# A first-pass weight product as a 2x3 by 3x3 block product in 15 products instead of a 2x2 by 2x2 one in 7, with chained banks and a ring of operands

## The chip, the cores and the metric

The kernel runs on one core of a Trainium2 chip. The metric is the device time of one execution in microseconds, taken on the chip; the profile is of one execution by the hardware profiler. The engines are named PE (TensorE), DVE (VectorE), ACT (ScalarE), POOL (GpSimd) and SP (SyncE, here only a queue for transfers).

## The reference

The input is 128 graphs of 64 nodes with 768 features each, and an adjacency matrix of whole numbers per graph. Two layers follow each other, each of the form x = x + layer(relu(layernorm(x))).

```python
def layer0(h, adj):
    radj = swapaxes(adj, 1, 2)
    deg, rdeg = adj.sum(-1), radj.sum(-1)          # zeros replaced by 1 in the divisions
    ctx = (adj @ (h @ Wadj.T + badj)) / deg
    ctx = ctx + (radj @ (h @ Wrev.T + brev)) / rdeg
    ctx = ctx + h @ Wself.T + bself
    agg = einsum('bij,bijr->bir', adj, E[adj])     # E[rels] with rels = adj
    rel = agg @ Wr.T + br * deg
    rr = where(radj + 40 > 40, radj + 40, 0)
    ragg = einsum('bij,bijr->bir', radj, E[rr])
    return ctx + rel + ragg @ Wrr.T + brr * rdeg

def layer1(h, adj):                                # six heads of 128
    z = einsum('bni,hio->bhno', h, W)
    a = leaky(src(tanh(z)) + dst(tanh(z)).T)       # masked where adj == 0
    f = elu(softmax(a) @ z + b)
    g = sigmoid(h @ H_w.T + H_b)
    return g * f + (1 - g) * h
```

Layer 0 has three 768x768 products for every node (Wadj, Wrev, Wself). They dominate the first pass, and they are what the change rewrites.

## The kernel before, in words

Two graphs make a tile of 128 rows by 768 columns; there are 64 tiles, handled in NP = 32 pairs. A first pass does layer 0 for all pairs, a second pass layer 1; between them h of layer 1 and x + h go through memory (H1D and XH1).

**Operands of the first pass.** For each tile, layernorm and relu give h (ACT, L331). TensorE multiplies blocks of h by the graph's matrices A/deg, Aᵀ/rdeg and the identity (L422, output in PSUM under the name pb), so that the features come out transposed, with nodes in columns, as a left operand for the three weights. ACT copies these blocks from PSUM to SBUF (L434, L440). All three weights are summed into the same PSUM bank, so a product of one row block with one column block is a chain of matmuls over (block of the inner dimension, weight).

**The product before.** Per pair the two tiles are two row blocks, and the 768 inner rows and 768 columns are each halved. This 2x2 by 2x2 block product is done in Winograd's form with 7 products instead of 8. Each product is KH = 3 inner blocks times 3 weights = 9 matmuls of 128x384 in fp32 (L466), so 63 for a pair, which the trace shows as 126 records (an fp32 matmul leaves two). Four banks, pwa to pwd, take them. The sums of operands that the form wants are s1 and s3 by DVE (L441, L442, one input still in PSUM) and s2 and s4 by POOL (L447, L452); the sums of weights, twelve tiles of 1152 columns, are made once at the start by DVE (L184). DVE adds every finished bank to x (L483, eight adds of 128x384 a pair).

**Counts.** The relation terms depend only on how often each value is found in a row of the adjacency matrix. DVE compares (L378), masks (L383) and reduces (L385), makes digits (L390 to L396), POOL copies them (L401), TensorE transposes them (L409), ACT copies those (L411), and a short bf16 matmul with a table (L475) adds the relation terms to the banks.

**End of a pair.** finish(p) runs beside the next pair's products: statistics by DVE (L159 to L165), a power on POOL (L166), the small DVE operation L167 for the second factor, relu by ACT to hf (L524), the store of hf, x + hf by POOL (L526), the store of x.

**Order of the work.** main(p) lists a pair's matmuls as numbered steps. side(p+1) lists the next pair's preparation with step numbers, and merged() issues each side piece at its number; the scheduler of the framework then settles the order on each engine. Each engine works its own queue in order and waits on the others by semaphores. Buffers are taken from rings: x and h1 share one ring of eight tiles of 128x768. fetch() brings the second pass's weights during the last pair of the first pass.

**Second pass.** Transposes of h (L646), seven products with two weights (L675), the attention (L753, L810, L819, L835), and the final L849 to L852.

Of the kernel before, what the change touches and what calls it, by code (L numbers as in the profile page):

```python
# [15 lines left out]
P = 128  # L16
EPS = 1e-5
NEG_MASK = -999.0
LEAKY = 0.2


@with_exitstack
def kernel(
# [47 lines left out]

    nc = tc.nc
# [11 lines left out]
    HALF = D // 2  # L84
    HH = H // 2
# [9 lines left out]
    assert GT == 2 and N == 64 and DO == P and H == KB and KB % 2 == 0 and H % 2 == 0  # L95
# [76 lines left out]
    def block(name, mats, place):  # L172
        return [keep.tile([P, KH, HALF], F32, name=f"{name}{s}", tag=f"w{place}{s}") if s < 2 else
                keep.tile([P, KH, HALF], F32, name=f"{name}{s}", tag="wl", bufs=7)
                for s in range(mats)]


    SUMS = {"T1": ("T3", "11"), "T2": ("22", "T1"), "T4": ("21", "T2"), "T3": ("22", "T3")}

    def sum_of_weights(w, to, behind=False):  # L180

        a, b = SUMS[to]
        for s, t in enumerate(w[to]):
            ins = nc.vector.tensor_sub(t, w[a][s], w[b][s])  # L184
            if behind:
                tc.keep_in_program_order(ins)


    bv, H1 = {}, {}

    def load_h(p):
        for k in range(2):
            t = 2 * p + k
            H1[t] = keep.tile([P, D], F32, name="h1", tag="x", bufs=8)
            nc.sync.dma_start(H1[t], H1D[p][k * P : (k + 1) * P, :])

    def fetch():

        def blk_of(name, place, h, q):
            bv[name] = block(f"bv{name}", 2, place)  # L200
            for s, src in enumerate((w_cat, hw_t)):
                nc.sync.dma_start(
                    bv[name][s],
                    src[h * HALF : (h + 1) * HALF, q * HALF : (q + 1) * HALF].rearrange(
                        "(k p) n -> p k n", p=P))

        def own(name, place):
            bv[name] = block(f"bv{name}", 2, place)

        return [(4, lambda: load_h(0)),  # L210
                (9, lambda: blk_of("11", "11", 0, 0)),
                (19, lambda: blk_of("21", "21", 1, 0)),
                (28, lambda: blk_of("T3", "T1", 0, 1)),
                (37, lambda: blk_of("22", "T2", 1, 1)),
                (47, lambda: (own("T1", "T4"), sum_of_weights(bv, "T1"), sum_of_weights(bv, "T3"))),
                (58, lambda: (own("T2", "T3"), sum_of_weights(bv, "T2")))]


    with ExitStack() as px:
# [7 lines left out]
        def load(p):  # L227
# [7 lines left out]
            for t in (2 * p, 2 * p + 1):  # L235
                X[t] = keep.tile([P, D], F32, name="x", bufs=8)
                nc.sync.dma_start(X[t], xf[t * P : (t + 1) * P, :])

        load(0)
# [3 lines left out]
        bia = work.tile([5, D], F32, name="bia", tag="s3")  # L243
        for i, v in enumerate((br, brr, badj, brev, bself)):
            nc.scalar.dma_start(bia[i : i + 1, :], row(v, 1))


        bw = {n: block(f"bw{n}", 3, n) for n in ("11", "21", "22", "T1", "T2", "T3", "T4")}

        def load_block(to, h, q):  # L250
            for s, src in enumerate((wadj_t, wrev_t, wself_t)):
                nc.sync.dma_start(
                    to[s], src.rearrange("(k h p) n -> h p k n", h=2, p=P)[h][:, :, q * HALF : (q + 1) * HALF])

        load_block(bw["11"], 0, 0)
        load(1)
        load_block(bw["21"], 1, 0)
        load_block(bw["T3"], 0, 1)
        load_block(bw["22"], 1, 1)
        wrt = work.tile([P, 2, D], F32, name="wrt", tag="a1")  # L260
        nc.sync.dma_start(wrt[:, 0, :], wr_t)
        nc.sync.dma_start(wrt[:, 1, :], wrr_t)
# [22 lines left out]
        def build_table():  # L285
# [21 lines left out]
            for hf in range(2):  # L307
                s = slice(hf * HALF, (hf + 1) * HALF)
                for d in range(2):
                    nc.tensor.matmul(pt[:NROW, hf, :HALF], es[:, d, :], wrt[:, d, s],  # L310
                                     start=(d == 0), stop=False)
                nc.tensor.matmul(pt[:NROW, hf, :HALF], eb, bia[:, s], start=False, stop=True)
            v = work.tile([P, D], F32, name="tv", tag="eq", bufs=1)
            qs = work.tile([P, 3, D], BF16, name="tq", tag="a22")
            nc.scalar.copy(v[:NROW].rearrange("p (a b) -> p a b", a=2), pt[:NROW, :, :HALF])
            for i in range(3):
                q = qs[:, i]
# [7 lines left out]
        A1, A22, S1, S2, S3, S4 = {}, {}, {}, {}, {}, {}  # L325
# [87 lines left out]
        def operands(p, k, q):  # L413
# [12 lines left out]
            pv = ps[:, :, : 6 * N].rearrange("p g (x n) -> p g x n", n=N)  # L426

            def blocks(ap):
                return ap.rearrange("p s (g n) -> p g s n", g=GT)

            if k == 0:
                if q == 0:
                    A1[p] = work.tile([P, KH, 2, 3, P], F32, name="a1")
                nc.scalar.copy(A1[p][:, q].rearrange("p h s (g n) -> p g (h s) n", g=GT), pv)  # L434
                return
            if q == 0:
                A22[p] = work.tile([P, KH, 3, P], F32, name="a22")
                S1[p] = work.tile([P, KH, 3, P], F32, name="s1", bufs=1)
                S3[p] = work.tile([P, KH, 3, P], F32, name="s3")
            nc.scalar.copy(blocks(A22[p][:, q]), pv[:, :, 3:])  # L440
            nc.vector.tensor_sub(blocks(S3[p][:, q]), blocks(A1[p][:, q, 0]), pv[:, :, :3])  # L441
            nc.vector.tensor_add(blocks(S1[p][:, q]), blocks(A22[p][:, q]), pv[:, :, :3])  # L442

        def sum2(p):
            S2[p] = work.tile([P, KH, 3, P], F32, name="s2", bufs=1)
            for q in range(KH):
                nc.gpsimd.tensor_sub(S2[p][:, q], S1[p][:, q], A1[p][:, q, 0])  # L447

        def sum4(p):
            S4[p] = work.tile([P, KH, 3, P], F32, name="s4", bufs=1)  # L450
            for q in range(KH):
                nc.gpsimd.tensor_sub(S4[p][:, q], A1[p][:, q, 1], S2[p][:, q])  # L452

        def main(p):

            bank = {}
            x0, x1 = X[2 * p], X[2 * p + 1]
            steps = []

            def mm(b, a, w, first):  # L460
                for q in range(KH):
                    for s in range(3):
                        def step(q=q, s=s):
                            if first and q == s == 0:
                                bank[b] = psw.tile([P, 512], F32, name=f"pw{b}")
                            nc.tensor.matmul(bank[b][:, :HALF], a()[:, q, s, :], bw[w][s][:, q, :],  # L466
                                             start=(first and q == s == 0),
                                             stop=(q == KH - 1 and s == 2),
                                             skip_group_check=True)
                        steps.append(step)  # L470

            def counts(b, k, q):
                def step():
                    for i, (a, e) in enumerate(PARTS):
                        nc.tensor.matmul(bank[b][:, :HALF], CT_T[p, k][: 3 * (e - a), i, :],  # L475
                                         tabs[i][:, q * HALF : (q + 1) * HALF],
                                         start=False, stop=True, skip_group_check=True)
                steps.append(step)

            def add(xt, q, b):  # L480
                def step():
                    v = xt[:, q * HALF : (q + 1) * HALF]
                    nc.vector.tensor_add(v, bank[b][:, :HALF], v)  # L483
                last = steps[-1]
                steps[-1] = lambda: (last(), step())

            mm("a", lambda: A1[p][:, :, 0], "11", True)
            add(x0, 0, "a")
            mm("c", lambda: A1[p][:, :, 1], "21", True)
            if p:  # L490
                counts("c", 0, 0)
                add(x0, 0, "c")
            mm("b", lambda: S1[p], "T1", True)
            add(x1, 1, "b")
            mm("a", lambda: S2[p], "T2", False)
            add(x0, 1, "a")
            mm("d", lambda: A22[p], "T4", True)
            if p:
                counts("d", 1, 0)
                add(x1, 0, "d")  # L500
            mm("a", lambda: S3[p], "T3", False)
            add(x1, 0, "a")
            mm("b", lambda: S4[p], "22", False)
            n = len(steps)
            counts("a", 1, 1)
            add(x1, 1, "a")
            if p:
                steps.insert(n - 4, steps.pop())
            else:
                counts("c", 0, 0)  # L510
                add(x0, 0, "c")
                counts("d", 1, 0)
                add(x1, 0, "d")
            counts("b", 0, 1)
            add(x0, 1, "b")
# [13 lines left out]
        def side(p):  # L529

            if p >= NP:
                return []
            return [(4, lambda: load(p + 1)),
# [3 lines left out]
                    (6, lambda: prep_r(p)),  # L537
                    (10, lambda: count(p, 0)),
                    (18, lambda: operands(p, 0, 0)),
# [424 lines left out]
```

## Time and profile before

| what | value |
|---|---|
| time before, median of 3 | 2593.01 us (2592.85 to 2593.08) |
| span of the profiled execution | 2591.5 us |
| busy: PE, DVE, ACT, POOL | 2543.7, 1765.7, 856.6, 733.4 us |
| from one pair to the next, first pass | 47.36 us |
| from one pair to the next, second pass | 31.66 us |
| start of pair 1 of the first pass | 89.88 us |
| first transpose of the second pass | 1554.08 us |

The busy figures are sums over the whole span and over stages with different limits. The period of a pair is taken from the starts of the first product in the chain of waits, and the last two rows divide the span into the start-up with pair 0, the 31 other pairs of the first pass, and the second pass. Where a matmul is followed by another, its time on TensorE is best read from start to start, as the records overlap.

### The profile page before, as it was taken

The page shows a single profiled execution, that of the slowest core. Times are in us where ns is not written, and L with a number is a line of the kernel's source. Part 1 is how long each engine was busy: PE and PEld are TensorE (multiplying, and loading weights), DVE is VectorE, ACT ScalarE, POOL GpSimd, SP SyncE. Part 2 cuts the span into 40 slices and gives each one's busy share as a digit, 9 for nine tenths or more (in the row PEclk, how much of TensorE's full clock was granted, in tenths as well). Part 3 has the DMA queues.
Part 4 walks back from the last instruction along what each step waited for, and adds up shares of the span by engine and source line. Part 5 has one row for each costly group of instructions (what it writes and reads, how often), then busy time and mean ns, then how long its engine had stood idle before and what let it go on. Part 6 is the DMA issues. An engine that isn't in the chain of part 4 may idle for free.

```text
span 2591.5 us, 31957 instructions
## 1 busy us (share of the span) xinstructions
PE 2543.7 (98%) x10924; PEld 1525.5 (59%) x10924; DVE 1765.7 (68%) x3887; ACT 856.6 (33%) x2596; POOL 733.4 (28%) x1055
## 2 busy tenths in 40 slices
PE   6999999999999999999999999999999999999996
PEld 3556666556566565565665655656566565565654
DVE  7856566565564665655655435888888888888888
ACT  1111112111111121111111104555555555555555
POOL 2331232232222312322223114333333333333332
PEclk9999999999999999999999999999999999999998
DMA  5112121121121111211211133333333333333322
GB/s 182 44 48 69 39 74 43 39 78 39 39 78 39 61 56 39 78 39 39 78 39 44 67 116 97 106 105 108 105 105 106 103 100 101 100 100 101 100 87 80
DMA packets 101572, 198.78 MB, mean 77 GB/s; under 512 B 35114, under 2 KB 43677, under 8 KB 101410
## 3 DMA queue, kind: packets, MB, share of 16 engines
q1 hardware_dynamic: 101256, 196.70, 23.9%
q8 instruction: 86, 1.41, 0.2%
q14 instruction: 76, 0.62, 0.1%
q10 hardware_dynamic: 154, 0.06, 0.0%
HBM read 95.67 MB, written 75.50 MB: 66 GB/s over the span
## 4 chain that ended last, share of the span: by engine, by line
PE 94%; DVE 3%; DMA 1%; ACT 1%; issue 1%; POOL 0%; SPq 0%; DVEq 0%; ACTq 0%; POOLq 0%
PE pwa L466 21%; PE pwb L466 14%; PE pma L675 14%; PE pmb L675 10%; PE pmc L675 9%; PE pwd L466 7%; PE pwc L466 7%; PE pb L422 5%; PE ps L835 2%; PE ps L646 2%; PE ps L819 1%; PE pwc L475 0%; DMA bw<-in_wadj_t_dram 0%; DVE bwT L184 0%; DMA x<-in_x_dram 0%
## 5 line engine op out<-in xcount | busy, mean ns | idle before, releaser
L466 PE MATMUL pwa<-bwT,s 128*128 128x384 f32 x1152 | 392.5, 490 | 0.4 <-DVE x L483 0.4
L466 PEld LDWEIGHTS pwa<-bwT,s 128*128 128x128 f32 x1152 | 215.5, 190 | 145.9 <-issue 8.0
L675 PE MATMUL pma<-bvT,s 128*128 128x384 f32 x768 | 279.4, 486 | 0.0
L447 POOL TENSOR_TENSOR s<-s,a 128x384 f32<-128x384 f32 x96 | 95.5, 1021 | 644.2 <-PE pwa L466 597.1
L483 DVE TENSOR_TENSOR x<-pwa,x 128x384 f32<-128x384 f32 x128 | 69.5, 543 | 206.8 <-PE pwa L466 170.7
L753 POOL TENSOR_TENSOR pr<-th,wsd 128x768 f32<-128x768 f32 x64 | 119.5, 1867 | 299.8 <-ACT th L751 236.6
L434 ACT COPY a<-pb 128x768 f32<-128x768 f32 x96 | 73.7, 801 | 392.3 <-PE pb L422 392.3
L466 PE MATMUL pwb<-bw,s 128*128 128x384 f32 x576 | 201.5, 489 | 0.0
L466 PE MATMUL pwb<-bwT,s 128*128 128x384 f32 x576 | 199.0, 491 | 0.0
L466 PE MATMUL pwa<-bw,a 128*128 128x384 f32 x576 | 196.2, 489 | 0.0
L466 PE MATMUL pwc<-bw,a 128*128 128x384 f32 x576 | 191.3, 486 | 0.0
L466 PE MATMUL pwd<-bwT,a 128*128 128x384 f32 x576 | 191.3, 486 | 0.0
L411 ACT COPY cntT<-pb 117x128 bf16<-117x128 bf16 (+1 forms) x128 | 27.8, 269 | 484.4 <-PE pb L409 484.4
L675 PEld LDWEIGHTS pma<-bvT,s 128*128 128x128 f32 x768 | 140.0, 190 | 80.8 <-DVE z L701 0.2
L422 PE MATMUL pb<-r,h 64*128 64x192 f32 x1536 | 153.8, 339 | 13.2 <-ACT h L331 6.7
L422 PEld LDWEIGHTS pb<-r,h 64*128 64x128 f32 x1536 | 124.5, 189 | 71.0 <-issue 52.9
L466 PEld LDWEIGHTS pwc<-bw,a 128*128 128x128 f32 x576 | 109.4, 190 | 76.6 <-issue 0.6
L466 PEld LDWEIGHTS pwd<-bwT,a 128*128 128x128 f32 x576 | 109.4, 190 | 76.3 <-issue 0.2
L675 PE MATMUL pmb<-bv,s 128*128 128x384 f32 x384 | 150.7, 502 | 0.0
L466 PEld LDWEIGHTS pwa<-bw,a 128*128 128x128 f32 x576 | 106.7, 191 | 69.4 <-issue 8.4
L466 PEld LDWEIGHTS pwb<-bwT,s 128*128 128x128 f32 x576 | 106.1, 190 | 69.1 <-issue 6.7
L675 PE MATMUL pmb<-bvT,s 128*128 128x384 f32 x384 | 144.3, 486 | 0.0
(155 smaller groups left out, 4723.1 us busy)
## 6 DMA issues: line engine op xcount, KB each, us to landing
x<-in_x_dram SPq DMA_DIRECT2D x64, 384.0 KB
h<-hf SPq DMA_DIRECT2D x64, 384.0 KB
xh<-x SPq DMA_DIRECT2D x64, 384.0 KB
h<-h SPq DMA_DIRECT2D x64, 384.0 KB
x<-xh SPq DMA_DIRECT2D x64, 384.0 KB
hx<-hs SPq DMA_DIRECT2D x128, 192.0 KB
out_dram<-f SPq DMA_DIRECT2D x62, 384.0 KB
ai<-in_adj_dram SPq DMA_DIRECT2D x64, 64.0 KB
```

The lines of the kernel that those rows point to most:

```text
L411: nc.scalar.copy(cn[: 3 * (b - a), i, :], pn[: 3 * (b - a), i, :])
L422: nc.tensor.matmul(ps[:, g, i * 3 * N : (i + 1) * 3 * N], H0[t][s, kb * P : (kb + 1) * P], rts[p % 2][s, k].rearrange("p s n -> p (s n)"), ...
L434: nc.scalar.copy(A1[p][:, q].rearrange("p h s (g n) -> p g (h s) n", g=GT), pv)
L447: nc.gpsimd.tensor_sub(S2[p][:, q], S1[p][:, q], A1[p][:, q, 0])
L466: nc.tensor.matmul(bank[b][:, :HALF], a()[:, q, s, :], bw[w][s][:, q, :], start=(first and q == s == 0), stop=(q == KH - 1 and s == 2), sk ...
L483: nc.vector.tensor_add(v, bank[b][:, :HALF], v)
L646: nc.tensor.transpose(ps[:, i, :], H1[2 * p + k][:, kb * P : (kb + 1) * P], ident)
L675: nc.tensor.matmul(bank[b, s][:, :HALF], a[p][:, q, :], bv[w][s][:, q, :], start=(first and q == 0), stop=(q == KH - 1), skip_group_check= ...
L753: nc.gpsimd.tensor_mul(pr, th, wsd[:, 0, :].rearrange("p (h o) -> p h o", h=H))
L819: nc.tensor.transpose(ps[:, c, :], PB[t][:, 2 * c : 2 * c + 2, :].rearrange("p h n -> p (h n)"), ident)
L835: nc.tensor.matmul(po[r][o, c, :], PT[t][s, c, o], (HS if r == g else HX)[t][s, 2 * c + r, :], start=True, stop=True)
```

## The change

The two tiles of a pair stay the two row blocks, but the inner dimension and the columns are now cut into three parts of 256. The 2x3 by 3x3 block product takes 18 products in the plain way, and 15 here. Each product is KQ = 2 inner blocks times 3 weights = 6 matmuls of 128x256, so 90 matmuls or 180 records a pair. It is for doing the same product with fewer columns streamed through TensorE: 90×256 = 23040 instead of 63×384 = 24192.

What comes with it:

- Operand sums. Eleven sums f1 to f11 of the operand blocks (A_SUMS), each 128x768, by DVE, in place of s1 to s4. f5 alone starts with a minus sign, and goes as a scalar_tensor_tensor. Six plain copies from PSUM by ACT make a00 to a12.
- Weight sums. Thirteen (B_SUMS) of 128x1536 at the start, in place of twelve of 1152, some written over their own inputs.
- Chained banks. Each bank takes one product after another without being cleared, and after each product its whole content is added to one block of x, or subtracted from it. Products that share a partial sum so share a bank. There are 16 adds of 128x256 a pair (15 products, and the counts of block 12 by themselves), in place of eight of 384. Banks a and b carry most of the chain in turn.
- A ring of operands, `op`, of 18 buffers, of which a pair takes 17.
- One region of SBUF, `weights`, of 15×1536 columns, for all weights of the first pass; the second pass's weights and some of its tiles (HS, HX, hbb) take over parts of it.
- The ring of x and h1 has six tiles instead of eight, and load(p+1) moves from step 4 to step 24. The numbers of the other side pieces move with the new order of products.
- At the end of the second pass the last two swaps are steps of their own.

```diff
+PRODUCTS = (
+    ("f1", "g6", "a", True, "11", "+", False),
+    ("f7", "g10", "b", True, "00", "-", False),
+    ("f4", "b21", "a", False, "01", "-", False),
+    ("a00", "g12", "b", False, "01", "-", False),
+    ("a02", "g14", "a", False, "00", "-", False),
+    ("f9", "g9", "b", False, "02", "+", False),
+    ("f6", "g5", "a", False, "02", "+", False),
+    ("a01", "b11", "d", True, "01", "+", True),
+    ("f8", "g3", "b", False, "12", "-", False),
+    ("f5", "b22", "a", False, "12", "-", False),
+    ("a11", "g1", "b", False, "11", "+", True),
+    ("f2", "g11", "a", False, "10", "+", True),
+    ("f3", "g8", "c", True, "12", "-", False),
+    ("f11", "b10", "d", True, "00", "+", True),
+    ("f10", "b12", "c", False, "02", "+", True),
+)
...
-            nc.scalar.copy(blocks(A22[p][:, q]), pv[:, :, 3:])
-            nc.vector.tensor_sub(blocks(S3[p][:, q]), blocks(A1[p][:, q, 0]), pv[:, :, :3])
-            nc.vector.tensor_add(blocks(S1[p][:, q]), blocks(A22[p][:, q]), pv[:, :, :3])
+            a = OPS[p, f"a{k}{q}"] = work.tile([P, KQ, 3, P], F32, name="op", bufs=18)
+            nc.scalar.copy(a.rearrange("p h s (g n) -> p g (h s) n", g=GT),
+                           ps[:, :, : 6 * N].rearrange("p g (x n) -> p g x n", n=N))
+        def form(p, *names):
+            for n in names:
+                s0, x, s1, y = A_SUMS[n]
+                t = OPS[p, n] = work.tile([P, KQ, 3, P], F32, name="op", bufs=18)
+                signed(t, s0, OPS[p, x], s1, OPS[p, y])
...
+            def add(b, c, sign="+"):
+                k, q = int(c[0]), int(c[1])
+                v = X[2 * p + k][:, q * CQ : (q + 1) * CQ]
+                if sign == "+":
+                    nc.vector.tensor_add(v, bank[b][:, :CQ], v)
+                else:
+                    nc.vector.tensor_sub(v, v, bank[b][:, :CQ])
+            def product(an, bn, b, first, c, sign, cnt):
+                def step(q, s):
+                    if first and q == s == 0:
+                        new(b)
+                    nc.tensor.matmul(
+                        bank[b][:, :CQ], OPS[p, an][:, q, s, :],
+                        bw[bn][:, (s * KQ + q) * CQ : (s * KQ + q + 1) * CQ],
+                        start=(first and q == s == 0), stop=(q == KQ - 1 and s == 2),
+                        skip_group_check=True)
+                    if q == KQ - 1 and s == 2:
+                        if cnt and p:
+                            counts(b, c)
+                        add(b, c, sign)
...
-            return [(4, lambda: load(p + 1)),
+            return [(24, lambda: load(p + 1)),
...
-                    (6, lambda: prep_r(p)),
-                    (10, lambda: count(p, 0)),
...
+                    (9, lambda: prep_r(p)),
+                    (15, lambda: count(p, 0)),
+                    (30, lambda: count(p, 1)),
+                    (40, lambda: digits(p)),
+                    (54, lambda: operands(p, 1, 2)),
+                    (54, lambda: operands(p, 1, 1)),
+                    (66, lambda: form(p, "f1")),
+                    (66, lambda: operands(p, 0, 0)),
+                    (66, lambda: operands(p, 0, 2)),
+                    (72, lambda: form(p, "f7", "f4")),
+                    (77, lambda: operands(p, 1, 0)),
+                    (77, lambda: operands(p, 0, 1)),
+                    (82, lambda: form(p, "f8", "f9", "f2")),
+                    (86, lambda: count_t(p, 0)),
+                    (86, lambda: count_t(p, 1)),
+                    (89, lambda: form(p, "f5", "f6", "f3", "f10", "f11"))]
```

## The prediction

> **What bounds the kernel now.** I read the page's first two parts, then the chain that ended last, the windows by stage, and the groups of a steady stretch of the first pass. The page first:
>
> ```profile
> PE 2543.7 (98%) x10924; PEld 1525.5 (59%) x10924; DVE 1765.7 (68%) x3887; ACT 856.6 (33%) x2596; POOL 733.4 (28%) x1055
> PE   6999999999999999999999999999999999999996
> PE 94%; DVE 3%; DMA 1%; ACT 1%; issue 1%; POOL 0%; SPq 0%; DVEq 0%; ACTq 0%; POOLq 0%
> ```
>
> TensorE is busy for 98% of the span, in every slice, and the chain is TensorE for 94%. An average hides stages, so the windows (PE, PEld, DVE, ACT, POOL busy, then the granted clock):
>
> ```profile
> 73.00:120.00 47.00, 45.25 (x184) 26.85 (x183) 38.51 (x98) 10.22 (x20) 17.02 (x19) 1.00 0.17 57
> 120.00:594.00 474.00, 474.00 (x1873) 285.05 (x1872) 285.15 (x614) 83.90 (x141) 121.97 (x140) 1.00 0.16 53
> 594.00:1068.00 474.00, 474.00 (x1872) 284.95 (x1872) 276.00 (x601) 82.91 (x140) 121.73 (x141) 1.00 0.16 53
> 1600.00:2000.00 400.00, 400.00 (x1959) 239.76 (x1958) 336.75 (x748) 233.69 (x859) 130.81 (x221) 1.00 0.33 100
> ```
>
> In the steady first pass TensorE never pauses: 474.00 of 474.00 us, at full clock. DVE has 40% to spare (285.15 of 474). The chain shows the first product of a pair starting at 126.55 and 173.90, so a pair takes 47.36 us. A change there pays what it takes from TensorE, as long as DVE, which has to empty the banks, keeps up. The groups of the stretch 300 to 1490 us:
>
> ```profile
> L466 PE MATMUL pwa<-bwT,s 128*128 128x384 f32 x912 | 309.1, 489 | 0.0
> L159 DVE BATCH_NORM_STATS2 st<-x 128x6 f32<-128x384 f32 x197 | 100.5, 551 | 2.6
> L385 DVE TENSOR_REDUCE sum<-eq 128x26 f32<-128x1664 bf16 x49 | 92.1, 1880 | 0.8
> L526 POOL TENSOR_TENSOR x<-x,hf 128x768 f32<-128x768 f32 x50 | 89.6, 1818 | 0.9 <-ACT hf L524 0.9
> L447 POOL TENSOR_TENSOR s<-s,a 128x384 f32<-128x384 f32 x75 | 72.7, 999 | 513.9 <-PE pwa L466 513.9
> L483 DVE TENSOR_TENSOR x<-pwa,x 128x384 f32<-128x384 f32 x100 | 54.2, 542 | 162.1 <-PE pwa L466 139.1 <-PE pwa L475 22.9
> L167 DVE SCALAR_TENSOR_TENSOR rn<-mv,rn 128x1 f32<-128x1 f32 x98 | 54.1, 552 | 59.7 <-POOL rn L166 59.7
> L441 DVE TENSOR_TENSOR s<-a,pb 128x384 f32<-128x384 f32 x76 | 41.7, 549 | 82.7 <-ACT a L440 82.7
> ```
>
> The matmuls wait for nothing. The suspicious group is L167: one element per partition, yet 552 ns on average. The timeline has the reason:
>
> ```profile
> 616.98 0.16 DVE L167 SCALAR_TENSOR_TENSOR rn<-mv,rn 128x1 f32<-128x1 f32 x1 [0.29 <-POOL rn L166]
> 617.49 1.76 DVE L167 SCALAR_TENSOR_TENSOR rn<-mv,rn 128x1 f32<-128x1 f32 x1 [0.36 <-POOL rn L166]
> ...
> 617.41 3.60 POOL L526 TENSOR_TENSOR x<-x,hf 128x768 f32<-128x768 f32 x2
> ```
>
> 0.16 us normally, 1.76 us when it starts inside POOL's first x += h: it ends when that ends. Of 24 such starts in the stretch all 24 stretched.
>
> **What the Trainium skill says.** (1) "SBUF — State Buffer", section "Who interferes with whom": DVE and GpSimd share a port pair under an exclusive lock. The trace agrees for operations with two SBUF inputs (L167, above) and for fast casts (L336 took 1.91 us inside L526, 0.29 outside); the adds L483, with one input in PSUM, show no stretching. (2) "TensorE: Matmul & The Clock Gate", section "Wait — 56ns, not 53.3ns?": N columns take N/2.4 + 2.5 ns from start to start. An fp32 matmul is two records here; records of L466 start 322 ns apart, which is 2×384/2.4 + 2.5. So 256 columns should take 216 ns. No 256-column fp32 matmul is in the trace, but 128x128 fp32 ones start 109 ns apart with their weight loads, so a load is no bound at 216. (3) "VectorE: DVE Perf Modes", section on the TRN2 errata: an fp32 add of N takes (N+151)/0.96 ns. The trace agrees: 1152 elements 1.344 us (L184, unlocked), 384 from PSUM 0.558.
>
> **TensorE's part.** A pair had 126 records of 384 columns: 126×0.3225 = 40.64 us. It gets 180 of 256: 180×0.2158 = 38.84. Counts: 8×0.166 = 1.33 become 12×0.110 = 1.32. The operand matmuls L422 stay (3 groups of 16, 1.717 us each with entry and exit, 5.15), small ones 0.33. Before: 47.45 (measured 47.36, so the sum is sound). After: 45.64. That is −1.7 us a pair, if TensorE never waits.
>
> **DVE's part.** A pair had 28.6 us (285.15 over the ten pairs of a window). Removed: six sums L441/L442 and eight adds L483, 14×0.55 = 7.7; 20.9 stay. Added: 11 sums of 768, each taking the queue for 0.87 (1152 starts 1.27 apart; 384 fewer at 0.96 GHz takes off 0.40), 9.6 us; 16 adds of 256, by the same step from 384 (0.465 apart) 0.335, or 0.38 with waits, 6.1. DVE comes to about 37 us of a pair of 46 to 48: 80%. POOL loses twelve operations of 1.0 us, the x += h stays. ACT's copies stay about level (six of 0.80 for four of 0.80 and four of 0.48) and hide.
>
> **The new wait.** Before, one to three products on other banks lay between two uses of a bank, each 5.8 us (18×0.3225). Now products alternate a, b, a, b..., each accumulating on the bank's old content, and each is added to x before the next but one may write. A product is 12×0.2158 = 2.59 us. From a product's end, DVE sees it after 0.20 us (as L483 does), the add takes 0.43, TensorE sees that after 0.05: 0.68. So an add may be 1.9 us late; later, TensorE stands and everything behind on its queue with it. DVE works in order. Between adds the order of the changed program puts blocks of 2.5 to 3.6 us: normalisation (recip 1.67, rd 0.41), dense counts (3.6), compare-and-reduce (2.9), three sums (2.6). One block over 2.59 only eats slack; several in a row overrun it.
>
> I worked one pair through by hand, with these durations, from the first product's start (0). The tail of the pair before has nine sums in the last six product times, so DVE arrives 2.0 us late (last add and f11). Statistics and A1, the first product's add, run to 4.3. The pow releases rn0 at 4.6, hf by ACT to 5.9, x += h on POOL from 6.1 to 7.9. rd and recip run to 7.2, then rn1 has two SBUF inputs and is locked to 7.9. A2 ends at 8.5 where product 4 could have begun at 7.9: 0.6 lost. The second x += h runs 9.2 to 11.0; the casts af, ab fall in it and A3 goes from 8.9 to 11.5: product 5 loses 0.46. Then dense counts, 3.1 us before A4: product 6 loses 0.9. Compare and reduce, 2.8 us: product 7 loses 0.6. After that DVE is in time until the sums at the end. Lost: 2.6 us; with ct2's 0.1, period 45.67 + 2.7 = 48.4. Leaving out all locks gives 46.05; locking only two-input operations, not casts, 47.2; moving durations and latencies by a tenth of a microsecond gives 47.0 to 48.9. I take 47.9, below the fully locked figure as not every cast will meet a POOL operation: +0.55 a pair over 47.36. Over 30 steady pairs +16.
>
> **The ends.** Start-up: twelve weight sums of 1152 become 13 of 1536 (1.67 against 1.27), and 11 sums of pair 0 join in the same queue; the sums fill DVE from about 18 to 50 us and the first add stands behind them. Pair 1 started at 89.9; I estimate 90 to 95, +3. The last pair has no side work: 40.2 against 41.9, −1.7. Second pass: no product is changed and the order of TensorE, DVE and ACT is the same. The ring of X and H1 has six buffers for eight: h1 of the next pair can be asked for when the fused L850 lets go, in the trace at 2026.95 and 2035.02; first needed at 2039.42, a load lands in about 3 us, so it hides behind product matmuls with 1.4 us to spare. load(p+1) in the first pass moves later, after finish(p−1); a store-to-load is 2.4 to 2.9 us in the trace, x is needed at the statistics ten microseconds later: hidden. The single region for weights costs nothing in the steady state (weights arrive under 90 matmuls of the last pair); the start-up figure holds its risk. Sum: 2593.0 + 16 + 3 − 1.7 ≈ 2610.
>
> **Rivals.**
> (1) Sums and adds all hidden. For it: DVE 80%, 40% was free; against it: the blocks between adds, and L167's 1.76. Period 46.0: 30×(−1.35) − 1.7 + 2 = −40; with none at all lost (45.65), −51. Time 2542 to 2553.
> (2) Partly hidden: casts escape the lock, or the adds come earlier than I laid them; period 46.4 to 47.2. 30×(−0.55) = −17, −1.7, +3: about 2577.
> (3) DVE worse than thought: chains of sums (each reads the one before), locks and PSUM access all at the upper end, period 48.9: 30×1.54 = +46, +5, −2: 2642. For it: f-sums and weight sums are wholly two-input.
> (4) The second pass waits for h1 or x from the smaller ring: 31 pairs by up to 0.5 us, +15 on any of these. For it: 1.4 us spare only.
>
> **How the numbers follow.** Chances: forecast (47.5 to 48.4) 0.38, rival 3 with 4 added 0.12, rival 2 0.22, rival 1 0.20, and 0.08 in the strip around no change (period 47.3 to 47.45). Slower by over 0.2%: 0.38 + 0.12 = 0.50; within 0.2%: 0.08; faster: 0.42. The low end 2545 takes in most of rival 1, the high end 2645 rival 3.
>
> **What would show it.** Right: TensorE's busy share in the steady windows falls from 100% to about 95%, with idle before the main products released by DVE's adds, at products 4 to 7 of each pair; records 216 ns apart; DVE near 37 us a pair; L167's counterpart still stretched, and casts beside x += h. Wrong, to rival 1: windows at 100% and pair starts 45.7 us apart. Wrong otherwise: records of 256 columns over 225 ns (weight loads bind: each 0.01 us is 1.8 us a pair); waits at operand copies by ACT; idle in the second pass's first transposes.

## The result and the profile after

The changed kernel takes 2608.26 us (median of 4 runs, 2607.93 to 2608.99) against 2592.99 for the kernel before: a ratio of 1.0059, 95% interval 1.0042 to 1.0077. It is slower by 15 us. The page of the changed kernel, busy times and the chain that ended last, and then its windows (PE, PEld, DVE, ACT, POOL busy in each), with the lines that answer to those of before:

```profile
PE 2519.4 (97%) x12780; PEld 1855.7 (71%) x12780; DVE 2024.9 (78%) x4309; ACT 887.4 (34%) x2596; POOL 588.4 (23%) x863
...
PE 65%; DVE 26%; issue 5%; ACT 1%; DMA 1%; POOL 1%; SPq 0%; POOLq 0%; DVEq 0%; ACTq 0%
```

```profile
120.00:594.00 474.00, 462.03 (x2424) 383.56 (x2424) 362.79 (x747) 91.93 (x139) 81.05 (x82) 1.00 0.16 53
594.00:1068.00 474.00, 462.26 (x2434) 383.58 (x2433) 351.93 (x720) 92.64 (x140) 79.67 (x79) 1.00 0.16 53
1600.00:2000.00 400.00, 400.00 (x1923) 239.95 (x1922) 332.51 (x757) 231.98 (x849) 131.66 (x233) 1.00 0.31 98
```

TensorE's share of the span hardly fell (98% to 97%), but its share of the chain fell from 94% to 65%, and DVE's rose from 3% to 26%. The share of busy time hides what the chain tells. In a steady window of the first pass TensorE now stands for 12 of 474 us, in the second pass for none. DVE went from 60% to 77% (362.79 of 474). It still idles for a quarter of the time and yet is what TensorE waits for.

The pair period is 47.80 us, against 47.36. The span's 14.9 us divide so: start-up to the first product of pair 1, +1.5 (89.88 to 91.43); the 30 pairs up to the last, +13.1; the last pair, −1.2; the second pass, +1.4, of which 1.0 is one wait at its first products. In the second pass the pairs start 31.65 us apart in both kernels.

Where in a pair the time goes, TensorE's timeline shows (start, duration; in brackets the idle time and what ended it). The first line is product 1 of a pair:

```profile
667.52 2.75 PE L546 MATMUL pwa<-weights,op 128*128 128x256 f32 x12
...
672.82 2.75 PE L546 MATMUL pwa<-weights,op 128*128 128x256 f32 x12
676.01 2.86 PE L546 MATMUL pwb<-weights,op 128*128 128x256 f32 x12 [0.45 <-DVE x L540]
678.71 2.75 PE L546 MATMUL pwa<-weights,op 128*128 128x256 f32 x12
681.87 2.86 PE L546 MATMUL pwb<-weights,op 128*128 128x256 f32 x12 [0.41 <-DVE x L540]
685.05 2.86 PE L546 MATMUL pwa<-weights,op 128*128 128x256 f32 x12 [0.32 <-DVE x L540]
```

Take the starts: product 4 begins 3.19 us after product 3, products 6 and 7 begin 3.16 and 3.18 after the ones before, where 2.59 is a product's own time. Each wait was ended by an add, L540. What held the adds, DVE's and POOL's timelines show:

```profile
673.05 1.75 DVE L451 RECIPROCAL rd<-rd 128x256 f32<-128x256 f32 x1
674.72 0.91 DVE L227 SCALAR_TENSOR_TENSOR rn<-mv,rn 128x1 f32<-128x1 f32 x1
675.55 0.41 DVE L540 TENSOR_TENSOR x<-x,pwb 128x256 f32<-128x256 f32 x1
...
677.60 1.18 DVE L434 TENSOR_SCALAR ov<-ab 128x256 bf16<-128x256 bf16 x1
...
681.40 0.41 DVE L540 TENSOR_TENSOR x<-x,pwb 128x256 f32<-128x256 f32 x1
681.73 1.02 DVE L463 TENSOR_TENSOR eq<-eq,wo 128x1664 bf16<-128x1664 bf16 x1
682.78 1.89 DVE L465 TENSOR_REDUCE sum<-eq 128x26 f32<-128x1664 bf16 x1
684.59 0.41 DVE L540 TENSOR_TENSOR x<-x,pwa 128x256 f32<-128x256 f32 x1
```

```profile
673.80 1.81 POOL L576 TENSOR_TENSOR x<-x,hf 128x768 f32<-128x768 f32 x1
676.82 1.87 POOL L576 TENSOR_TENSOR x<-x,hf 128x768 f32<-128x768 f32 x1 [1.21 <-ACT hf L574]
```

The second L227 begins at 674.72, inside POOL's first x + h, and ends with it at 675.6: 0.91 us for what takes 0.16. L434 begins at 677.60, inside the second, and ends with it at 678.7: 1.18 for 0.22. The add of product 2 stands behind the first, that of product 4 behind the second. That add also has a compare ahead of it, and the add of product 5 comes after mask and reduce (L463, L465). DVE's order is what the timeline lists; none of the late adds waited for its own product.

### The profile page after: what moved, and what is told of

Its sections match the earlier page's. It is cut to its first block, busy times and chain, and to the rows that moved or that the text cites. A ratio compares the mean times of both kernels' runs of the same rounds, so it can differ in the third digit from the quotient of the medians.

```text
span 2606.4 us, 36038 instructions
## 1 busy us (share of the span) xinstructions
PE 2519.4 (97%) x12780; PEld 1855.7 (71%) x12780; DVE 2024.9 (78%) x4309; ACT 887.4 (34%) x2596; POOL 588.4 (23%) x863
## 4 chain that ended last, share of the span: by engine, by line
PE 65%; DVE 26%; issue 5%; ACT 1%; DMA 1%; POOL 1%; SPq 0%; POOLq 0%; DVEq 0%; ACTq 0%
PE pma L727 14%; PE pwa L546 10%; PE pmb L727 10%; PE pmc L727 9%; DVE op L245 7%; PE pwb L546 6%; PE pb L502 4%; PE pwd L546 3%; PE pwc L546 3%; DVE sum L465 2%; DVE x L540 2%; PE ps L887 2%; DVE st L219 2%; PE ps L698 2%; DVE eq L458 1%
## 5 line engine op out<-in xcount | busy, mean ns | idle before, releaser
L546 PE MATMUL pwa<-weights,op 128*128 128x256 f32 x2304 | 540.6, 384 | 12.1 <-DVE x L540 12.1
L546 PEld LDWEIGHTS pwa<-weights,op 128*128 128x128 f32 x2304 | 429.1, 191 | 92.3 <-DVE x L540 23.9
L546 PE MATMUL pwb<-weights,op 128*128 128x256 f32 x1920 | 451.4, 383 | 29.7 <-DVE x L540 25.0
L245 DVE TENSOR_TENSOR op<-op 128x768 f32<-128x768 f32 x320 | 305.4, 985 | 193.8 <-ACT op L507 193.8
L546 PEld LDWEIGHTS pwb<-weights,op 128*128 128x128 f32 x1920 | 355.3, 190 | 101.2 <-DVE x L540 48.3
L727 PE MATMUL pmb<-weights,s 128*128 128x384 f32 x768 | 295.1, 494 | 1.0 <-DVE s L712 1.0
L727 PE MATMUL pmc<-weights,a 128*128 128x384 f32 x768 | 285.4, 488 | 0.0
L727 PE MATMUL pma<-weights,s 128*128 128x384 f32 x768 | 279.4, 486 | 0.0
L481 POOL COPY c<-cnt 128x243 bf16<-128x243 bf16 x64 | 47.8, 776 | 733.5 <-PE pb L489 672.0
L546 PE MATMUL pwc<-weights,op 128*128 128x256 f32 x768 | 197.7, 389 | 10.8 <-DVE weights L243 10.8
L546 PE MATMUL pwd<-weights,op 128*128 128x256 f32 x768 | 176.9, 379 | 0.0
L502 PE MATMUL pb<-r,h 64*128 64x192 f32 x1536 | 153.5, 339 | 8.2 <-ACT h L411 8.1
L502 PEld LDWEIGHTS pb<-r,h 64*128 64x128 f32 x1536 | 124.7, 189 | 39.7 <-issue 27.3
```

Of the source, the lines that this page charges most:

```text
L245: return (nc.vector.tensor_add if s1 == "+" else nc.vector.tensor_sub)(to, x, y)
L502: nc.tensor.matmul(ps[:, g, i * 3 * N : (i + 1) * 3 * N], H0[t][s, kb * P : (kb + 1) * P], rts[p % 2][s, k].rearrange("p s n -> p (s n)"), ...
L546: nc.tensor.matmul(bank[b][:, :CQ], OPS[p, an][:, q, s, :], bw[bn][:, (s * KQ + q) * CQ : (s * KQ + q + 1) * CQ], start=(first and q == s ...
L727: nc.tensor.matmul(bank[b, s][:, :HALF], a[p][:, q, :], bv[w][s][:, q, :], start=(first and q == 0), stop=(q == KH - 1), skip_group_check= ...
```

## The experiments

Two theories stood against each other. By the prediction, TensorE waits because DVE is late at certain places: POOL's lock and blocks of other work come just before adds that must be in time. The rivals: DVE is simply too full (volume), or chained banks cost TensorE time whatever DVE does.

**The sum x + h left out.**

```diff
-                nc.gpsimd.tensor_add(X[t], X[t], h)
```

> This kernel leaves out the sum x + h at the end of a pair (POOL, L576), so the residual h of the second layer is missing; the stores stay. Theory (late DVE, made late by POOL's lock): the two stretched DVE operations of a pair, the second L227 (0.91 us, 0.16 unlocked) and the first L434 (1.18, 0.22 unlocked), fall back, 1.7 us come off the DVE queue just where products 4, 6 and 7 wait for its adds (2.0 us a pair in the changed kernel). The period falls from 47.80 to 46.0 to 46.3, the time to 2555 to 2565. Rival A (DVE is late by the volume of its work and the place of its blocks, the lock is incidental): the stalls at products 6 and 7 stay, period 47.3 or more, time 2593 or more. Rival B (the chained banks cost TensorE time whatever DVE does): period unchanged, 2608.

Measured: 2552.02 us, ratio to the kernel before 0.9839 (0.9823 to 0.9856), period 45.82. Two groups between 300 and 1490 us (busy and mean ns of one after the first bar), first of the changed kernel and then of this one, and a window of this one:

```profile
L227 DVE SCALAR_TENSOR_TENSOR rn<-mv,rn 128x1 f32<-128x1 f32 x100 | 34.8, 348 | 27.4 <-POOL rn L226 27.4
L434 DVE TENSOR_SCALAR ov<-ab 128x256 bf16<-128x256 bf16 x24 | 28.3, 1178 | 0.0
...
L227 DVE SCALAR_TENSOR_TENSOR rn<-mv,rn 128x1 f32<-128x1 f32 x100 | 14.1, 141 | 11.4 <-POOL rn L226 11.4
L434 DVE TENSOR_SCALAR ov<-ab 128x256 bf16<-128x256 bf16 x24 | 5.3, 219 | 0.0
```

```profile
120.00:594.00 474.00, 474.00 (x2544) 402.78 (x2545) 351.71 (x761) 96.83 (x146) 38.49 (x62) 1.00 0.16 53
```

L227 and L434 are back at 141 and 219 ns, and TensorE is busy for 474.00 of 474.00 us. The banks alternate as before, so the chaining as such costs nothing: that rival falls. The period fell by 1.98 us for 1.8 us of DVE time freed by these two (a pair has four of L227 and one of L434). But the run is not a test of the lock alone, because the scheduler also ordered DVE's work otherwise. Mask and reduce, which stand ahead of the add of product 5 in the changed kernel, come behind it here:

```profile
613.63 0.40 DVE L540 TENSOR_TENSOR x<-x,pwa 128x256 f32<-128x256 f32 x1
...
614.16 0.97 DVE L463 TENSOR_TENSOR eq<-eq,wo 128x1664 bf16<-128x1664 bf16 x1
...
615.17 1.89 DVE L465 TENSOR_REDUCE sum<-eq 128x26 f32<-128x1664 bf16 x1
```

What the new order is worth can be estimated. In the changed kernel that add ends 17.5 us into its pair; with 1.8 us less ahead of it, it would end at 15.7. Product 7 starts at 15.65 here, so with the old order it would be about 0.1 us late. Most of the 1.98 us is then the lock's, but no run shows the split.

**The sum x + h on DVE, where DVE idles.** `finish_x` is split off and comes at step 60; the load follows it. The first statistics of the next pair's h are held at steps 30 and 36, so more than the sum moves.

```diff
-                nc.gpsimd.tensor_add(X[t], X[t], h)
+        def finish_x(p):
+                ins = nc.vector.tensor_add(X[t], X[t], HF[t])
+                tc.keep_in_program_order(ins)
...
+            more = [(3, lambda: finish(p - 1)), (60, lambda: finish_x(p - 1))]
-            return [(24, lambda: load(p + 1)),
+            return [(66, lambda: load(p + 1)),
-                    (0, lambda: norm(2 * p)),
-                    (0, lambda: norm(2 * p + 1)),
+                    (30, lambda: norm(2 * p)),
+                    (36, lambda: norm(2 * p + 1)),
```

> The sum x + h is done by DVE, fixed behind the add of product 10, where DVE idles for some 11 us a pair between products 9 and 13; the load of x comes at step 66, and the first statistics of h are held at steps 30 and 36. DVE gets 1.75 us more work a pair, POOL loses 3.6. Theory (lock and place): as without the sum, period 46.0 to 46.4, time 2555 to 2568. Rival A (volume of DVE work): no gain or a loss, period 47.8 or more, time 2608 or more.

Measured: 2574.96 us, ratio 0.9929 (0.9914 to 0.9944), period 46.71. The direction is that of the theory, and volume as the cause falls: DVE has more work and the kernel is 33 us faster. The size misses the expected range. A stall of 0.6 us stayed at product 4, although nothing was locked there. DVE's timeline from the pair's first add shows another cause:

```profile
703.40 0.41 DVE L538 TENSOR_TENSOR x<-pwa,x 128x256 f32<-128x256 f32 x1
704.20 0.16 DVE L227 SCALAR_TENSOR_TENSOR rn<-mv,rn 128x1 f32<-128x1 f32 x1 [0.40 <-POOL rn L226]
...
704.75 0.55 DVE L219 BATCH_NORM_STATS2 st<-x 128x6 f32<-128x384 f32 x1
705.56 0.16 DVE L227 SCALAR_TENSOR_TENSOR rn<-mv,rn 128x1 f32<-128x1 f32 x1 [0.26 <-POOL rn L226]
705.63 1.75 DVE L451 RECIPROCAL rd<-rd 128x256 f32<-128x256 f32 x1
707.30 0.36 DVE L540 TENSOR_TENSOR x<-x,pwb 128x256 f32<-128x256 f32 x1
```

The edit held only one half of the first statistics at its step. The other half (L219 at 704.75) slid ahead of the add of product 2, and the reciprocal went behind L227 and its wait for POOL: 0.55 + 0.26 us in the same place where the lock had been.

**The counts moved.** The compare, mask and reduce groups go about two products later (by the timelines of one pair in each kernel, 5.5 and 4.4 us), and the compares of all pairs but the first are held at their steps; x + h stays on POOL.

```diff
-            if p < 2 and k == 0:
+            if p:
                 tc.keep_in_program_order(ins)
...
-                    (15, lambda: count(p, 0)),
-                    (30, lambda: count(p, 1)),
-                    (40, lambda: digits(p)),
+                    (36, lambda: count(p, 0)),
+                    (54, lambda: count(p, 1)),
+                    (62, lambda: digits(p)),
```

> The two compare, mask and reduce groups of a pair move on DVE, with no work added or taken: the first from products 4 and 5 to products 7 and 8, the second to products 10 and 11. POOL's x + h stays, and with it the lock. Theory: the stalls at products 6 and 7 (1.26 us a pair) vanish, the one at product 4 (0.73) stays, since the lock on L227 comes before it: period 46.5, time about 2570. Rival A' (the lock alone matters): little change, 2600 or more. Rival B (chained banks): 2608.

Measured: 2567.47 us, ratio 0.9899 (0.9885 to 0.9914), period mostly 46.16. No work was added or taken, L227 and L434 were still stretched (353 and 1179 ns on average), and the stalls at products 6 and 7 went. At product 4 a stall of 0.25 us stayed, and product 5 started 0.1 us late after it. What had been expected to stay was 0.73, the two together as in the changed kernel. The difference comes from the other end of the pair: the copies of the counts on POOL (L481) no longer run beside the operand sums, whose mean falls from 988 to 954 ns over ten a pair, so DVE comes into the next pair earlier. The first product of a pair and the add of its product 2 show it:

```profile
604.30 2.75 PE L546 MATMUL pwa<-weights,op 128*128 128x256 f32 x12
611.96 0.41 DVE L540 TENSOR_TENSOR x<-x,pwb 128x256 f32<-128x256 f32 x1
```

The add begins 7.66 us after the product, where it is 8.03 in the changed kernel (667.52 and 675.55), with the same operations ahead of it: 0.37 us, which is what the stall lost. The second lock (L434) can be borne when no block follows it.

**Both edits.**

> Both edits: x + h by DVE behind product 10, and the counts moved. Theory: all three stalls vanish, the period is that of TensorE's own work, 45.7 to 46.0, time 2545 to 2556, below the kernel before (2593). Rival A (volume): above 2590. Rival B (chained banks): near 2608.

Measured: 2558.98 us, ratio 0.9866 (0.9851 to 0.9880), period 46.17. The half of the statistics that was not held was left in it, with a stall of 0.25 us at product 4, and the expected range is missed by 3 us.

**Both edits, and both halves of the statistics held.**

```diff
-            if behind and i == 0:
+            if behind:
                 tc.keep_in_program_order(ins)
```

> As the kernel with both edits, but both halves of the first statistics of h are held behind product 5, so that none of them (0.55 us) runs ahead of the add of product 2. Theory (in-order DVE, the place of each piece counts): the stall of 0.36 us a pair at product 4, which was left there, vanishes; period 45.8, time 2559 - 30 x 0.36 = 2548, range 2544 to 2552. Rival: something else than DVE's lateness holds product 4, period 46.17 as before, 2559.

Measured: 2548.33 us, ratio 0.9827 (0.9812 to 0.9841), period 45.82. The chain of this kernel from its page, and two of its windows:

```profile
PE 95%; DVE 2%; DMA 1%; ACT 1%; issue 1%; POOL 1%; SPq 0%; DVEq 0%; POOLq 0%; ACTq 0%
```

```profile
120.00:594.00 474.00, 474.00 (x2546) 402.60 (x2545) 367.96 (x772) 98.01 (x146) 29.92 (x62) 1.00 0.17 57
594.00:1068.00 474.00, 474.00 (x2528) 403.27 (x2527) 369.95 (x786) 97.62 (x146) 30.30 (x62) 1.00 0.16 55
```

TensorE is without a pause again with DVE at 78%, more than in the changed kernel. This version leaves no work out, and is faster than the changed kernel and, by 45 us, than the one before.

**The sum x + h still on POOL, but later.** With both halves of the statistics held as above, but POOL does the sum, queued behind the powers of the first statistics; the counts stay at their steps.

```diff
+                ins = nc.gpsimd.tensor_add(X[t], X[t], HF[t])
+                tc.keep_in_program_order(ins)
...
+            more = [(3, lambda: finish(p - 1)), (38, lambda: finish_x(p - 1))]
```

> The sum x + h stays on POOL with its full work, but is queued behind the powers of the first statistics, some 22 us into the pair (product 8) instead of 6; the counts stay in products 4 to 8. Volume on DVE and POOL is as in the changed kernel, only the time of the lock moves to where DVE idles. Theory (lock at the wrong place): the second L227 at 0.16 us and L434 at 0.22, the three stalls vanish or nearly, period 45.8 to 46.1, time 2548 to 2560. Rival (volume, or the chained banks as such): period 47.5 or more, 2600 or more.

Measured: 2573.31 us, ratio 0.9922 (0.9905 to 0.9938), period 46.57. The stalls at products 4 and 6 are gone as expected, with the lock gone from there; the rest of the expectation misses: as the timeline reads, the lock was not harmless in its new place. DVE's timeline, then the waits of PE over ten pairs (total us, times, longest):

```profile
675.79 0.77 DVE L227 SCALAR_TENSOR_TENSOR rn<-mv,rn 128x1 f32<-128x1 f32 x1
676.48 0.41 DVE L538 TENSOR_TENSOR x<-pwd,x 128x256 f32<-128x256 f32 x1
676.82 1.54 DVE L470 CAST si<-sum 128x52 int32<-128x52 f32 x1
```

```profile
PE pb L502 <- ACT h L411: 3.5, 10, 0.3
```

L227 of the first statistics now meets the lock and stands behind a reduce. It releases h on ACT, and h the operand matmuls L502: TensorE waits for ACT in all ten pairs. Product 10 starts 4.60 us after product 9, instead of 4.18. A stall of 0.2 us stayed at product 7, where the counts are.

**Both edits, with x + h on POOL late.** The counts, the held statistics, and POOL at step 60 behind the powers.

> Counts moved, first statistics held, and x + h on POOL behind the powers. Theory: no stall, period 45.8, time 2544 to 2552, as with x + h on DVE, since TensorE sets the period in both. Rival: the lock, now beside the compare and mask of products 7 to 11, makes new stalls: 2560 or more.

Measured: 2548.83 us, ratio 0.9829 (0.9815 to 0.9844), period 45.82: as good as with DVE. The lock is there in every pair, and larger than ever. The groups, and a window:

```profile
L463 DVE TENSOR_TENSOR eq<-eq,wo 128x1664 bf16<-128x1664 bf16 x51 | 84.0, 1648 | 0.9
L227 DVE SCALAR_TENSOR_TENSOR rn<-mv,rn 128x1 f32<-128x1 f32 x102 | 54.5, 534 | 48.2 <-POOL rn L226 48.2
```

```profile
594.00:1068.00 474.00, 474.00 (x2529) 403.26 (x2528) 380.49 (x766) 97.81 (x146) 74.08 (x82) 1.00 0.17 55
```

L463 averages 1648 ns instead of 1016 and L227 534, DVE is busy for 80%, and TensorE loses nothing. In the changed kernel leaving the contention out saved 2 us a pair; here it costs nothing. It is the place that counts.

**The control: the kernel before without x + h.**

> The kernel before, without the sum x + h (POOL, L526); the residual h of the second layer is missing. Theory: there DVE had 40% to spare and TensorE was busy without a pause, so the lock cost nothing; L167 falls to 0.16 us, the period stays 47.36, time 2590 to 2594. Rival: the lock costs a pair 1.6 us wherever it falls: about 2545.

Measured: 2592.54 us, ratio 0.9998 (0.9989 to 1.0006), period 47.36. L227's counterpart fell from 552 to 159 ns, as its group shows; the window below it has TensorE without a pause, as before:

```profile
L167 DVE SCALAR_TENSOR_TENSOR rn<-mv,rn 128x1 f32<-128x1 f32 x98 | 15.6, 159 | 59.7 <-POOL rn L166 59.7
```

```profile
120.00:594.00 474.00, 474.00 (x1873) 285.06 (x1872) 269.02 (x614) 82.88 (x140) 86.93 (x121) 1.00 0.15 53
```

The lock was there all along and cost nothing while DVE had slack before every add. The change made it dear.

## Why the prediction was right

It forecast 2610 by a lost race between DVE's adds and the alternating banks, and 2608.26 was measured. Step by step:

- **TensorE's part** held. Twelve records of 256 columns take 2.59 us in the trace, 0.216 each, and a pair without stalls takes 45.82 against the 45.64 worked out. The gain was there, 1.54 us a pair where 1.7 was forecast, as the runs without stalls show.
- **DVE's part** held: about 37 us a pair were forecast; 362.79 us in 474 at a period of 47.80 are 36.6. The sum on record starts from 28.6 us a pair where 285.15 over ten pairs is 28.5, which changes nothing.
- **The new wait** was the right mechanism with the right releaser. The stalls were forecast at products 4, 5, 6 and 7 with 0.6, 0.46, 0.9 and 0.6, 2.6 in all; measured from start to start they are 0.6, 0.1, 0.6 and 0.6, and about 0.1 at product 8, 1.98 in all. The 0.1 at products 5 and 8 are no waits: a product that has waited takes 2.69 us to the next start instead of 2.59. TensorE's busy share fell to 97%, not to about 95%, because the records overlap and only 12 of 474 us show as idle. The first locked operation, L227, was the one forecast, and ended 8.1 us into the pair where 7.9 was forecast. The second was not: when the second x + h began at 676.82, the cast L416 was over and L420 had begun 0.09 us before and kept its 0.29, and L434 after them took 1.18 us. So the add of product 3 was in time and product 5 did not wait; the delay of 0.96 us went into the add of product 4.
- **The period** was taken as 47.9, below the full working of 48.4, on the ground that not every cast would meet the lock. The ground was right, but the size of the step, 0.5 us, was a judgement and not a sum: the working as it stood would have given about 2625 us. That the forecast came within 2 us is in part luck. The period is 47.80, and over the 30 pairs that is +13 instead of +16. The term without locks, 46.05, has its counterpart in the run without x + h, 45.82, where the order of DVE's work was another too.
- **The ends**: start-up +3 forecast, +1.5 measured; last pair −1.7 forecast, −1.2 measured; second pass nothing forecast, +1.4 measured. The smaller ring of X and H1 costs nothing in the steady second pass; what made the 0.4 us beside the one wait of 1.0 was not tried.

The terms forecast too high, +16 for +13.1 and +3 for +1.5, are partly cancelled by those forecast too low, −1.7 for −1.2 and 0 for +1.4. The rival "sums and adds all hidden", 2542 to 2553, is what the mended kernels reach, 2548.33 and 2548.83. The Trainium skill's rule on the shared port ("SBUF — State Buffer", "Who interferes with whom") agrees with these traces in what was looked at here: the operation that comes second waits to the end of the first (0.91 and 1.18 us), while the adds with an input in PSUM and the reductions that begin inside x + h keep their 0.41 us.

## What to carry to other kernels

An engine with a quarter of its time to spare can be the bound if others wait for single operations in its queue: before a change that shortens the time between a producer and the next use of its buffer, lay the other engine's queue beside the new deadlines, and see what stands directly ahead of each. A contention that costs nothing under slack is not gone, and a tighter schedule brings it to light; the cure is to move the contending piece to where the queue idles, on either engine. When moving one piece, look at what the scheduler puts into its place: here half a statistics operation in the wrong place cost 0.35 us a pair (46.17 against 45.82 once it was held).

## What the runs showed of the hardware that had not been expected

- The lock works the other way too. POOL's copies L481 average 799 ns in the changed kernel, where they run beside DVE's sums with two SBUF inputs, and 390 ns where the counts were moved away from them; each of two sums beside them takes 1.13 us instead of 0.96. The groups between 300 and 1490 us, of the changed kernel and of the one with the counts moved:

```profile
L481 POOL COPY c<-cnt 128x243 bf16<-128x243 bf16 x50 | 38.5, 799 | 580.3 <-PE pb L489 580.3
L481 POOL COPY c<-cnt 128x243 bf16<-128x243 bf16 x52 | 18.7, 390 | 201.9 <-DVE cnt L476 201.9
```
